# Graph attention layer after a masked attention layer: x1 gathered with (att + beta I) first, then the product with W, and token scores from x1 with a precomputed W a

## Chip, cores, metric

One core of a Trainium2 chip (trn2). The metric is device time in microseconds (us), median of several executions. Kernels are compared by the mean time of one kernel's fast runs over that of the other's fast runs of the same rounds, so a ratio is not quite the quotient of the medians quoted.

## The reference, cut to what matters

```python
# layer 0: 8-head attention over 256 tokens with an adjacency mask, residual, layer norm -> x1
x = _layernorm(x + _L0_gnn_ref(x, adj, Wq, bq, Wk, bk, Wv, bv, Wo, bo))
# layer 1, of x1 (64 batches, 256 tokens, 512 features)
h = jnp.einsum('bnc,cf->bnf', x, W)
s1 = jnp.einsum('bnf,f->bn', h, a1)
s2 = jnp.einsum('bnf,f->bn', h, a2)
e = jax.nn.leaky_relu(s1[:, :, None] + s2[:, None, :], negative_slope=0.2) * mask[None]
att = jax.nn.softmax(e, axis=2)
h_prime = jnp.einsum('bij,bjf->bif', att, h)
y = jax.nn.elu(h_prime + beta * h)
return _layernorm(x + y)
```

All is float32. With h = x1 W the layer is (att + beta I) x1 W, and s1 = x1 (W a1): that is what the change uses.

## The kernel before

Three batches are under way at a time. Each round of the loop runs the attention of one batch, the front (transposes, q, k, v) of the next and the back (projection, norm, layer 1, norm) of the one ahead, their steps merged by position: step i of a list of l steps stands at (i + 0.5) / l of the round.

```python
ps_mm = tile_pool(bufs=3, PSUM); ps_sc = tile_pool(bufs=2, PSUM); ps_tr = tile_pool(bufs=2, PSUM)

def merged(*lists):
    steps = [((i + 0.5) / len(l), k, f) for k, l in enumerate(lists) for i, f in enumerate(l)]
    return [f for _, _, f in sorted(steps, key=lambda s: s[:2])]

def layernorm(xt):                       # ... bn_stats, bn_aggr on VectorE
    nc.gpsimd.tensor_scalar(rs, mv[:, 1:2], EPS, None, ALU.add)
    nc.gpsimd.tensor_tensor(rs, rs, neg_half, ALU.pow)
    nc.vector.tensor_scalar(xt, xt, mv[:, 0:1], rs, ALU.subtract, ALU.mult)

def scores(t, g):                        # attention: 4 such steps a round
    for i in range(4): nc.tensor.matmul(ps[i % 2][...], QT..., KT...)       # two banks
    for s in range(2): nc.vector.tensor_add(pr[:, s::2, :], ps[s], mask)    # frees the banks
    nc.vector.tensor_reduce(nm, pr, AX.X, ALU.max, negate=True)
    for i in range(4): nc.scalar.activation(pr[:, i, :], ..., AF.Exp, bias=nm..., accum_out=sm...)
    nc.vector.reciprocal(rc, sm)
    nc.gpsimd.tensor_tensor(pr, pr, rc..., ALU.mult)    # 128x1024: "GpSimd's product" below
# flip(h): transposes of the probabilities, copied out by VectorE (even h) or ScalarE (odd h)
# mix(hp): two heads side by side, 4 matmuls of 64 columns of the array

def back(b):
    def proj(t):    # X += QT Wo, then
        layernorm(X[b][t])
    def flip(t):    # x1T = X transposed: 4 transposes and a copy
        transposed(X[b][t], t, x1T[0])
    def hidden(t):  # hs[t] = x1 W: 4 matmuls of 512 columns and a copy
        nc.scalar.copy(hs[t], ps)
        for i, v in enumerate((a1_sb, a2_sb)):
            nc.vector.scalar_tensor_tensor(junk, hs[t], 1.0, v, op0=ALU.mult, op1=ALU.mult,
                                           accum_out=s[t][:, i:i + 1])
    def edges(): ...      # s2 transposed on TensorE (tr_s), softmax of the edges over all engines
    def flip_att(): ...   # att transposed (tr_a)
    def last(t):    # ps = att hs, then
        nc.vector.scalar_tensor_tensor(u, hs[t], beta_sb, ps, op0=ALU.mult, op1=ALU.add)
        # ... elu(u), residual, layernorm, store
    return [proj, proj, flip, flip, hidden, hidden, edges, flip_att, last, last]   # for t = 0, 1
```

## Time and profile before

| | before |
|---|---|
| time | 3981.85 us (3980.74 to 3982.89, 4 runs) |
| a round of the loop | 61.44 us, 64 of them |
| TensorE busy | 94% |
| mean granted clock of TensorE | 0.945 |
| TensorE waits for the mask add ahead of a score step | 179.6 us, 2.87 us a round |

TensorE is busy almost always, and one wait stands out. The lines are in the prediction. A busy share counts modelled ends of pipelined instructions; for what an instruction costs on TensorE, the distance from its start to the next start is the better measure, and the one used here.

### The profile page before, as it was taken

The page shows a single profiled execution, that of the slowest core. Times are in us where ns is not written, and L with a number is a line of the kernel's source. Part 1 is how long each engine was busy: PE and PEld are TensorE (multiplying, and loading weights), DVE is VectorE, ACT ScalarE, POOL GpSimd, SP SyncE. Part 2 cuts the span into 40 slices and gives each one's busy share as a digit, 9 for nine tenths or more (in the row PEclk, how much of TensorE's full clock was granted, in tenths as well). Part 3 has the DMA queues.
Part 4 walks back from the last instruction along what each step waited for, and adds up shares of the span by engine and source line. Part 5 has one row for each costly group of instructions (what it writes and reads, how often), then busy time and mean ns, then how long its engine had stood idle before and what let it go on. Part 6 is the DMA issues. An engine that isn't in the chain of part 4 may idle for free.

```text
span 3978.9 us, 40466 instructions
## 1 busy us (share of the span) xinstructions
PE 3744.2 (94%) x15232; PEld 2258.9 (57%) x15232; DVE 2300.4 (58%) x4418; ACT 1147.1 (29%) x3265; POOL 924.5 (23%) x974
## 2 busy tenths in 40 slices
PE   7999999999999999999999999999999999999997
PEld 5555555556556555565555555555556556555563
DVE  3555565555655655656556555565555655655655
ACT  1332332322322323223222232332322322323222
POOL 2222221222222212222122222221222222212221
PEclk9999999999999999999999999999999999999998
DMA  2000000000000000000000000000000000000000
GB/s 93 13 20 22 11 22 16 17 22 11 22 22 11 22 16 17 22 11 22 20 14 22 14 19 22 11 22 16 16 22 11 22 22 11 22 17 16 16 6 16
DMA packets 40388, 76.26 MB, mean 19 GB/s; under 512 B 4352, under 2 KB 4608, under 8 KB 40192
## 3 DMA queue, kind: packets, MB, share of 16 engines
q1 hardware_dynamic: 37136, 67.39, 5.0%
q10 hardware_dynamic: 2640, 5.24, 0.4%
q8 instruction: 119, 1.95, 0.2%
q0 software_dynamic: 416, 1.05, 0.1%
q14 instruction: 77, 0.63, 0.1%
HBM read 40.11 MB, written 33.55 MB: 19 GB/s over the span
## 4 chain that ended last, share of the span: by engine, by line
PE 55%; DVE 22%; ACT 11%; POOL 7%; issue 4%; DMA 0%; POOLq 0%; SPq 0%; ACTq 0%; DVEq 0%
PE ps_qk L140 21%; PE ps_h L228 11%; ACT p L176 7%; PE tr_p L185 6%; PE ps_pv L197 5%; DVE nm L173 4%; PE ps_sc L168 4%; DVE x L120 3%; PE ps_g L269 3%; POOL rs L119 3%; PE tr_x L108 2%; DVE u L271 2%; DVE u L276 2%; DVE x L277 2%; DVE p L171 2%
## 5 line engine op out<-in xcount | busy, mean ns | idle before, releaser
L176 ACT ACTIVATE p<-p,nm 128x256 f32<-128x256 f32 x1024 | 507.6, 497 | 879.4 <-DVE nm L173 879.4
L179 POOL TENSOR_TENSOR p<-p,rc 128x1024 f32<-128x1024 f32 x256 | 484.6, 1893 | 903.8 <-DVE rc L178 903.8
L168 PE MATMUL ps_sc<-kT,qT 64*128 64x256 f32 x2048 | 388.2, 463 | 179.6 <-DVE p L171 179.6
L140 PE MATMUL ps_qk<-xT,wk_sb 128*128 128x256 f32 x2048 | 544.0, 413 | 0.0
L140 PE MATMUL ps_qk<-xT,wq_sb 128*128 128x256 f32 x2048 | 499.1, 387 | 0.3 <-ACT xT L109 0.3
L140 PEld LDWEIGHTS ps_qk<-xT,wk_sb 128*128 128x128 f32 x2048 | 417.3, 212 | 109.8 <-issue 53.5
L228 PE MATMUL ps_h<-w_sb,x1T 128*128 128x512 f32 x1024 | 473.1, 595 | 0.7 <-ACT x1T L109 0.7
L216 PE MATMUL ps_o<-wo_sb,qT 128*128 128x512 f32 x1024 | 460.8, 593 | 0.0
L146 PE MATMUL ps_v<-wv_sb,xT 128*128 128x512 f32 x1024 | 460.3, 592 | 0.0
L168 PEld LDWEIGHTS ps_sc<-kT,qT 64*128 64x128 f32 x2048 | 240.9, 215 | 351.6 <-DVE p L171 216.2
L140 PEld LDWEIGHTS ps_qk<-xT,wq_sb 128*128 128x128 f32 x2048 | 369.9, 190 | 85.8 <-issue 44.8
L120 DVE TENSOR_SCALAR x<-x,mv,rs 128x512 f32<-128x512 f32 x256 | 201.5, 787 | 316.7 <-POOL rs L119 316.7
L197 PE MATMUL ps_pv<-pT,v 128*64 128x256 f32 x2048 | 359.5, 393 | 0.3 <-DVE qT L199 0.3
L185 PE MATMUL tr_p<-ident,p 128*128 128x128 f32 x2048 | 350.8, 293 | 4.4 <-DVE pT L190 3.2
L190 DVE COPY pT<-tr_p 128x512 f32<-128x512 f32 x256 | 176.6, 690 | 306.4 <-PE tr_p L185 306.2
L171 DVE TENSOR_TENSOR p<-ps_sc,mask_sb 128x512 f32<-128x512 f32 x512 | 338.0, 672 | 22.8 <-PE ps_sc L168 22.8
L185 PEld LDWEIGHTS tr_p<-ident,p 128*128 128x128 f32 x2048 | 271.0, 151 | 117.4 <-issue 50.8
L146 PEld LDWEIGHTS ps_v<-wv_sb,xT 128*128 128x128 f32 x1024 | 194.4, 190 | 243.9 <-issue 243.9
L118 POOL TENSOR_SCALAR rs<-mv 128x1 f32<-128x1 f32 x256 | 56.1, 219 | 1113.1 <-DVE mv L116 1113.1
L173 DVE TENSOR_REDUCE nm<-p 128x4 f32<-128x1024 f32 x256 | 309.4, 1209 | 2.3
L246 POOL TENSOR_TENSOR e<-e,adj_sb 128x512 f32<-128x512 f32 x64 | 81.3, 1271 | 954.6 <-DVE e L245 954.6
L216 PEld LDWEIGHTS ps_o<-wo_sb,qT 128*128 128x128 f32 x1024 | 184.6, 190 | 185.2 <-issue 184.7
(56 smaller groups left out, 3746.1 us busy)
## 6 DMA issues: line engine op xcount, KB each, us to landing
x<-in_x_dram SPq DMA_DIRECT2D x128, 256.0 KB, 2.5
out_dram<-x SPq DMA_DIRECT2D x128, 256.0 KB, 2.0
wq_sb<-in_L_gnn_Wq_dram ACTq DMA_DIRECT2D x1, 1024.0 KB, 6.9
wk_sb<-in_L_gnn_Wk_dram ACTq DMA_DIRECT2D x1, 1024.0 KB, 14.6
wv_sb<-in_L_gnn_Wv_dram ACTq DMA_DIRECT2D x1, 1024.0 KB, 12.1
wo_sb<-in_L_gnn_Wo_dram ACTq DMA_DIRECT2D x1, 1024.0 KB, 8.6
w_sb<-in_L_gnn_W_dram ACTq DMA_DIRECT2D x1, 1024.0 KB, 9.9
a_sb<-in_L_gnn_a_dram POOLq DMA_DIRECT2D x2, 256.0 KB, 9.3
```

The lines of the kernel that those rows point to most:

```text
L120: nc.vector.tensor_scalar(xt, xt, mv[:, 0:1], rs, ALU.subtract, ALU.mult)
L140: nc.tensor.matmul(ps, w[:, c, m * P:(m + 1) * P], XT[b][:, c, :], start=c == 0, stop=c == C - 1)
L146: nc.tensor.matmul(ps, XT[b][:, c, t * P:(t + 1) * P], wv_sb[:, c, :], start=c == 0, stop=c == C - 1)
L168: nc.tensor.matmul(ps[i % 2][:, i // 2, :], QT[b][r:r + HD, h // 2, t * P:(t + 1) * P], KT[b][r:r + HD, h // 2, :], start=True, stop=True)
L171: nc.vector.tensor_add(pr[:, s::2, :], ps[s], mask_sb[:, t:t + 1, :].to_broadcast([P, 2, N]))
L173: nc.vector.tensor_reduce(nm, pr, AX.X, ALU.max, negate=True)
L176: nc.scalar.activation(pr[:, i, :], pr[:, i, :], AF.Exp, bias=nm[:, i:i + 1], accum_out=sm[:, i:i + 1])
L179: nc.gpsimd.tensor_tensor(pr, pr, rc.unsqueeze(2).to_broadcast([P, 4, N]), ALU.mult)
L185: nc.tensor.transpose(tr[:, k, t * P:(t + 1) * P], probs[t][:, h, k * P:(k + 1) * P], ident)
L197: nc.tensor.matmul(ps[s * HD:(s + 1) * HD, :], V[b][:, k, h * HD:(h + 1) * HD], pT[h][:, k, :], start=k == 0, stop=k == NT - 1)
L216: nc.tensor.matmul(ps, QT[b][:, c, t * P:(t + 1) * P], wo_sb[:, c, :], start=c == 0, stop=c == C - 1)
L228: nc.tensor.matmul(ps, x1T[0][:, c, t * P:(t + 1) * P], w_sb[:, c, :], start=c == 0, stop=c == C - 1)
```

## The change

The intent: spare the 8 transposes of x1 and the copies of h in each round by gathering x1 itself. TensorE can write (att + beta I) x1 straight in transposed form, which is what the product with W needs. The token scores then come from x1 and two vectors W a1, W a2 that are computed once. The diff, cut to its core (a helper line for each of beta_id and wa_sb, and removed comments, are left out):

```diff
+    wa_sb = const.tile([P, 2, C, P], F32, name="wa_sb")      # (W a1, W a2) on all partitions, once
 def proj(t):
     layernorm(X[b][t])
-def flip(t): ...
-def hidden(t): ...
+    for i in range(2):
+        nc.vector.scalar_tensor_tensor(junk, X[b][t], 1.0, wa_sb[:, i]..., accum_out=s[t][:, i:i + 1])
 def edges():
     nc.vector.tensor_scalar(e[:, t, :], e[:, t, :], rc[:, t:t + 1], None, ALU.mult)
+    nc.gpsimd.tensor_tensor(d, d, beta_id, ALU.add)          # d: the diagonal block of e
+def gather(g):                                               # y transposed: 4 matmuls of 256 columns
+    nc.tensor.matmul(ps[:, i, :], X[b][j][:, m * P:(m + 1) * P], att[1][:, j, :], ...)
+    nc.scalar.copy(yT[0][:, 2 * g:2 * g + 2, :], ps)
 def last(t):
-    nc.tensor.matmul(ps, att[1][:, j, t * P:(t + 1) * P], hs[j], ...)
-    nc.vector.scalar_tensor_tensor(u, hs[t], beta_sb, ps, op0=ALU.mult, op1=ALU.add)
+    nc.tensor.matmul(ps, yT[0][:, c, t * P:(t + 1) * P], w_sb[:, c, :], ...)
+    # relu, exp and max now read ps itself
-steps: proj, proj, flip, flip, hidden, hidden, edges, flip_att, last, last       (10)
+steps: proj, proj, edges, flip_att, gather, gather, last, last                   (8)
```

More of the change, by code (lines that the diff above doesn't have):

```diff
@@ L96, in gnn_two_layers @@
     beta_sb = on_all(beta, 0, 1, "beta_sb")
+    beta_id = const.tile([P, P], F32, name="beta_id")
+    nc.vector.tensor_scalar(beta_id, ident, beta_sb, None, ALU.mult)
     mask_sb = const.tile([P, NT, N], F32, name="mask_sb")
@@ L100, in gnn_two_layers @@
     nc.vector.tensor_scalar(mask_sb, mask_sb, NEG, None, ALU.mult)
+    wa_sb = const.tile([P, 2, C, P], F32, name="wa_sb")
+    for i, v in enumerate((a1_sb, a2_sb)):
+        row = ps_mm.tile([P, C, P], F32, tag="mm", name="ps_wa")
+        for c in range(C):
+            junk = work.tile([P, D], F32, tag="junk", name="junk")
+            col = small.tile([P, 1], F32, tag="wa", name="wa")
+            nc.vector.scalar_tensor_tensor(junk, w_sb[:, c, :], 1.0, v, op0=ALU.mult, op1=ALU.mult, accum_out=col)
+            nc.tensor.transpose(row[:, c, :], col.to_broadcast([P, P]), ident)
+        nc.scalar.copy(wa_sb[:, i], row)
     XT, QT, KT, V = {}, {}, {}, {}
@@ L210, in back @@
     def back(b):
-        hs, x1T, s, att = {}, {}, {}, {}
+        s, att, yT = {}, {}, {}
         def proj(t):
@@ L218, in proj @@
             layernorm(X[b][t])
-        def flip(t):
-            if t == 0:
-                x1T[0] = work.tile([P, C, N], F32, tag="x1T", name=f"x1T_{b}", bufs=1)
-            transposed(X[b][t], t, x1T[0])
-        def hidden(t):
-            ps = ps_mm.tile([P, D], F32, tag="mm", name="ps_h")
-            for c in range(C):
-                nc.tensor.matmul(ps, x1T[0][:, c, t * P:(t + 1) * P], w_sb[:, c, :], start=c == 0, stop=c == C - 1)
-            hs[t] = work.tile([P, D], F32, tag="h", name=f"h_{b}_{t}", bufs=4)
-            nc.scalar.copy(hs[t], ps)
             s[t] = small.tile([P, 2], F32, tag="s", name="s")
-            for i, v in enumerate((a1_sb, a2_sb)):
+            for i in range(2):
                 junk = work.tile([P, D], F32, tag="junk", name="junk")
-                nc.vector.scalar_tensor_tensor(junk, hs[t], 1.0, v, op0=ALU.mult, op1=ALU.mult,
-                                               accum_out=s[t][:, i:i + 1])
+                nc.vector.scalar_tensor_tensor(junk, X[b][t], 1.0, wa_sb[:, i].rearrange("p c k -> p (c k)"),
+                                               op0=ALU.mult, op1=ALU.mult, accum_out=s[t][:, i:i + 1])
         def edges():
@@ L255, in edges @@
                 nc.vector.tensor_scalar(e[:, t, :], e[:, t, :], rc[:, t:t + 1], None, ALU.mult)
+                d = e[:, t, t * P:(t + 1) * P]
+                nc.gpsimd.tensor_tensor(d, d, beta_id, ALU.add)
             att[0] = e
@@ L264, in flip_att @@
             nc.scalar.copy(att[1], tr)
-        def last(t):
-            ps = ps_mm.tile([P, D], F32, tag="mm", name="ps_g")
-            for j in range(NT):
-                nc.tensor.matmul(ps, att[1][:, j, t * P:(t + 1) * P], hs[j], start=j == 0, stop=j == NT - 1)
-            u = work.tile([P, D], F32, tag="u", name="u")
-            nc.vector.scalar_tensor_tensor(u, hs[t], beta_sb, ps, op0=ALU.mult, op1=ALU.add)
+        def gather(g):
+            if g == 0:
+                yT[0] = work.tile([P, C, N], F32, tag="yT", name=f"yT_{b}")
+            ps = ps_mm.tile([P, 2, N], F32, tag="mm", name="ps_y")
+            for i in range(2):
+                m = 2 * g + i
+                for j in range(NT):
+                    nc.tensor.matmul(ps[:, i, :], X[b][j][:, m * P:(m + 1) * P], att[1][:, j, :],
+                                     start=j == 0, stop=j == NT - 1)
+            nc.scalar.copy(yT[0][:, 2 * g:2 * g + 2, :], ps)
+        def last(t):
+            ps = ps_mm.tile([P, D], F32, tag="mm", name="ps_u")
+            for c in range(C):
+                nc.tensor.matmul(ps, yT[0][:, c, t * P:(t + 1) * P], w_sb[:, c, :], start=c == 0, stop=c == C - 1)
             m = work.tile([P, D], F32, tag="m", name="m")
-            nc.scalar.activation(m, u, AF.Relu, scale=-1.0)
+            nc.scalar.activation(m, ps, AF.Relu, scale=-1.0)
             nc.scalar.activation(m, m, AF.Exp, scale=-1.0)
-            nc.vector.scalar_tensor_tensor(u, u, 0.0, m, op0=ALU.max, op1=ALU.add)
-            nc.vector.scalar_tensor_tensor(X[b][t], u, -1.0, X[b][t], op0=ALU.add, op1=ALU.add)
+            nc.vector.scalar_tensor_tensor(m, ps, 0.0, m, op0=ALU.max, op1=ALU.add)
+            nc.vector.scalar_tensor_tensor(X[b][t], m, -1.0, X[b][t], op0=ALU.add, op1=ALU.add)
             layernorm(X[b][t])
             nc.sync.dma_start(out[b, t * P:(t + 1) * P, :], X[b][t])
-        steps = []
-        for f in (proj, flip, hidden):
-            steps += [lambda f=f, t=t: f(t) for t in range(NT)]
-        return steps + [edges, flip_att] + [lambda t=t: last(t) for t in range(NT)]
+        steps = [lambda t=t: proj(t) for t in range(NT)] + [edges, flip_att]
+        return steps + [lambda g=g: gather(g) for g in range(C // 2)] + [lambda t=t: last(t) for t in range(NT)]
     if B > 1:
```

## The prediction

> **What bounds the kernel now.** I read the page's engine totals, then the groups by form, then TensorE's timeline over several rounds of the loop, then the windows with the clock, then VectorE's timeline around the one stall that showed.
>
> ```profile
> PE 3744.2 (94%) x15232; PEld 2258.9 (57%) x15232; DVE 2300.4 (58%) x4418; ACT 1147.1 (29%) x3265; POOL 924.5 (23%) x974
> ...
> L168 PE MATMUL ps_sc<-kT,qT 64*128 64x256 f32 x2048 | 388.2, 463 | 179.6 <-DVE p L171 179.6
> ...
> L228 PE MATMUL ps_h<-w_sb,x1T 128*128 128x512 f32 x1024 | 473.1, 595 | 0.7 <-ACT x1T L109 0.7
> ```
>
> TensorE is the bound on average, but its only large idle time is 179.6 us ahead of the attention scores, waiting for VectorE to add the mask and so free the two score banks. The timeline shows this as one stall a round, always of the same length and 61.44 us apart:
>
> ```profile
> 2060.07 2.74 PE L168 MATMUL ps_sc<-kT,qT 64*128 64x256 f32 x8 [2.87 <-DVE p L171]
> 2121.51 2.73 PE L168 MATMUL ps_sc<-kT,qT 64*128 64x256 f32 x8 [2.87 <-DVE p L171]
> ```
>
> 64 rounds of 61.44 us are 3932 us; the other 50 us of the 3981.64 are start and end. The windows show that the stall costs more than its length (the column after POOL is the granted clock):
>
> ```profile
> 2056.00:2058.00 2.00, 1.20 (x6) 0.72 (x4) 1.97 (x3) 0.85 (x3) 0.00 (x0) 1.00 0.00 0
> 2058.00:2060.00 2.00, 0.00 (x0) 0.00 (x0) 1.18 (x4) 1.23 (x6) 0.48 (x1) 0.87 0.00 0
> 2060.00:2062.00 2.00, 1.93 (x7) 1.68 (x8) 0.68 (x3) 0.00 (x0) 1.92 (x3) 0.50 0.00 0
> 2062.00:2064.00 2.00, 2.00 (x9) 1.35 (x8) 1.72 (x3) 0.01 (x1) 0.25 (x1) 0.50 0.00 0
> 2064.00:2066.00 2.00, 2.00 (x8) 1.72 (x7) 2.00 (x4) 2.00 (x9) 0.00 (x0) 0.50 0.00 0
> 2066.00:2068.00 2.00, 2.00 (x14) 1.75 (x14) 1.80 (x4) 1.12 (x5) 1.65 (x1) 0.93 0.00 0
> ```
>
> From the fractions the half clock runs from 2059.5 to 2066.3. TensorE works through 6.2 us of it (2060.07 to 2066.3), so it loses 3.1 us. A round is then 55.4 us of work with its small gaps, 2.9 of stall and 3.1 of slow clock: 6 us, a tenth of the round, hangs on one wait. Its cause is on VectorE:
>
> ```profile
> 2045.77 1.55 DVE L120 TENSOR_SCALAR x<-x,mv,rs 128x512 f32<-128x512 f32 x1
> ...
> 2055.44 0.55 DVE L120 TENSOR_SCALAR x<-x,mv,rs 128x512 f32<-128x512 f32 x1 [2.71 <-POOL rs L119]
> 2055.91 1.21 DVE L173 TENSOR_REDUCE nm<-p 128x4 f32<-128x1024 f32 x1
> 2057.04 0.68 DVE L217 TENSOR_TENSOR x<-x,ps_o 128x512 f32<-128x512 f32 x1
> 2057.75 0.69 DVE L114 BATCH_NORM_STATS2 bn<-x 128x6 f32<-128x512 f32 x1
> 2059.26 0.18 DVE L178 RECIPROCAL rc<-sm 128x4 f32<-128x4 f32 x1 [0.82 <-ACT p L176]
> 2059.35 0.66 DVE L171 TENSOR_TENSOR p<-ps_sc,mask_sb 128x512 f32<-128x512 f32 x1
> ```
>
> In order, one score step's maximum waits behind a layer norm that waits 2.71 us for GpSimd; the exponentials wait for that maximum, the reciprocal for them, and the next mask add, which TensorE needs, stands behind the reciprocal. So the head of each round is a chain through VectorE; the rest of it is bound by TensorE.
>
> **What the Trainium skill says.** "TensorE: Matmul & The Clock Gate", Part 1, says the clock has two states, half and full, set by activity in free-running windows of about 3.4 us. The trace agrees: it falls to 0.50, and the drops at 2059.5, 339.2 and 219.7 us lie whole multiples of 3.413 us apart. An idle window of 2.28 us in 3.41 (67%) dropped the clock; the stall that ended at 278.85 lay across a window edge, 1.7 and 1.1 us, and the clock stayed at 1.00. The round of 61.44 us is also 18 such windows, so the kernel runs locked to the grid. The same page, section "Back-to-back issue gap", says that weight loads count as well as matmuls, and more at small widths; here 8 records of 256 columns take 1.73 us start to start and 8 of 512 take 3.43, and a 0.19 us load lies under each 0.216 us record, so halving the width costs nothing per column. "FP8 and Floating Point Precision", TensorE Precision Notes, says that true FP32 takes 4 passes; the trace agrees (a product of four 512-column matmuls, 3.43 us, is 16 times 0.214). "SBUF — State Buffer", section "Who interferes with whom", says that VectorE instructions with two SBUF inputs, or in the two-port mode, block against GpSimd; the norm's subtract and multiply shows it: 1.55 us beside a GpSimd add at 2045.77, 0.55 at 2055.44.
>
> **The change part by part, for one batch (a round).**
> TensorE: the 8 transposes of x1 go. Four take 0.44 us start to start (2006.12 to 2006.55), so 2 x 0.44 = 0.9 us. The product with W stays, 2 x 3.43 us. The product with the attention was 4 logical matmuls of 512 columns, 2 x 1.72 us; it becomes 8 of 256, 2 x 1.73. Net -0.9 us, all on the bound: 55.4 becomes 54.5.
> ScalarE: two copies of x1T (0.57) and two of h (0.59) go, two of yT (about 0.58, as other copies out of a bank) come: -1.2 us, on an engine that is 29% busy: nothing.
> VectorE: two beta*h+ps of 0.745 us go: -1.5 us. The two score reductions stay (0.69 + 0.08, twice for each block, 3.1 us) but move from the middle of the round, where VectorE idles, to straight behind the first norm, in the crowded head.
> GpSimd: two diagonal adds of 128x128 come, an estimate of 0.4 us each (a quarter of the 1.27 us of 128x512, plus a start cost), in the chain between the edges and the transposed attention.
> PSUM: the last product's bank is held through relu, exp and the max (0.63 + 0.63 + 0.69 us and queueing, about 3 us) instead of one read of 0.75. Between it and the third bank after it lie val, mix and the other last product, 3.4 + 1.0 + 3.4 us of TensorE: no wait expected.
> Order: the last stage loses 2 of 10 steps. By the program's spreading rule the second output projection now comes after the third score step, the edges right after the second projection's norm (between them q0, a score step, a flip and k0), and flip_att four steps on.
> Start: the new vectors W a need w_sb, issued at 18.2 us and landing 9.9 later, while the first q product ran at 21.05. If TensorE meets their transposes first, up to 13 us once; I take 10.
>
> **The head, walked by hand.** Relative to before: without the u instruction the last norm's VectorE work ends some 0.7 us earlier, before the first score step's mask add, not between its two halves beside GpSimd's bias add. The first maximum starts near 2046.5 instead of 2047.96, so everything up to the second mask adds comes 1.2 us earlier. The third score step is now only one transpose behind the second and waits about 0.5 us; the fourth, behind projection and q0 as before, waits about 1.2 us, plus 0.65 for its second bank. Against 2.87 + 0.65 before, that is better by about 1.2 us, and split. But then the edges need the second block's reductions, which stand in VectorE's queue behind the remaining score work: I expect 0 to 2.3 us of wait there, and 0 to 1.5 us at the transposed attention (its chain ran 5.9 us bare, 3918.22 to 3924.19, and has gained GpSimd work and busier neighbours). Sum of waits 2.5 to 6 us, middle 3.3, in three or four pieces. A piece over 2 us inside one window brings the half clock: 1.7 us for one window, 3.1 for two; middle 1.7.
> Round: 54.5 + 3.3 + 1.7 = 59.5 us; 64 x 59.5 = 3808, plus 50 and 10: **3868 us**, 2.9% less.
>
> **The rivals.**
> (a) The stalls split so that no window is mostly idle: 54.5 + 2.8 = 57.3 us, 3727 in all. For it: the stall at 278.85, and even a wait of 1.59 us ahead of the tr_p transposes at 284.98, left the clock at 1.00. Against: any one piece of 2 us undoes it.
> (b) The stall moves and the round stays locked at 18 windows, 61.44 us: about 3990 with the later start, so the saved 0.9 us is eaten. For it: the slow stretch ends on a grid edge wherever the stall lies, so a later stall end within it loses less clock, which pulls the round back to a multiple of 3.413. It needs waits and slow clock of 6.9 us together, which the walk reaches if the edges' wait is long.
> (c) VectorE becomes the head's bound: the work up to the transposed attention is, from the durations, about 25 us for VectorE against 19 for TensorE. Unless the order lets TensorE run q, k and flips ahead, two drops of clock follow and a round of 62.5 to 64: 4060 to 4160 us. Against: in the kernel before, such work did run ahead of the transposed attention, which waited 0.1 us.
> (d) Only the transposes count and stall and clock stay: 64 x 60.5 + 60 = 3932, within 2%.
>
> **Range and chances.** (a) at 25%, values between (a) and 3900 at 30%, (b) and (d) together at 33%, (c) at 12%. So faster by over 2% (under 3902) 0.55, within 2% 0.33, slower (over 4061) 0.12; range 3700 to 4000.
>
> **What would show it.** Right: no x1T transposes and TensorE's own work down by 0.9 us a round; product with attention 1.73 us per 8 records; waits of L168 split and shorter in total; granted clock above 0.945; first q product later by up to 13 us. The prediction is wrong if one new wait of over 3 us appears at the edges or the transposed attention, if the round is still 61.44 us, or if the product with the attention costs more per column than before.

## The result

| | before | after |
|---|---|---|
| time | 3981.85 us | 3966.69 us (3966.34 to 3967.94, 4 runs) |
| ratio | | 0.9963 (95%: 0.9949 to 0.9977) |
| mean round (59 rounds of the trace) | 61.42 us | 61.01 us |
| granted clock | 0.945 | 0.973 |
| wait ahead of score steps | 179.6 us | 29.3 us |
| wait ahead of the edge transposes | 1.9 us | 220.2 us |

The page's engine totals and two groups by form (columns: count, busy us, mean ns, then idle us before them and who ended it), of the kernel after:

```profile
PE 3637.0 (92%) x15240; PEld 2244.0 (57%) x15240; DVE 2231.8 (56%) x4307; ACT 1072.0 (27%) x3139; POOL 980.0 (25%) x1102
...
L181 PE MATMUL ps_sc<-kT,qT 64*128 64x256 f32 x2048 | 333.7, 402 | 29.3 <-DVE p L184 29.1
...
L241 PE MATMUL tr_s<-ident,s 128*128 128x128 f32 x128 | 40.2, 314 | 220.2 <-DVE junk L235 220.2
```

The wait that bounded the kernel before is nearly gone, and a larger one stands at the edges. TensorE's timeline after shows it in every round:

```profile
2006.50 0.32 PE L241 MATMUL tr_s<-ident,s 128*128 128x128 f32 x1 [3.38 <-DVE junk L235]
2067.77 0.32 PE L241 MATMUL tr_s<-ident,s 128*128 128x128 f32 x1 [3.37 <-DVE junk L235]
2127.98 0.48 PE L241 MATMUL tr_s<-ident,s 128*128 128x128 f32 x1 [3.37 <-DVE junk L235]
```

These two rounds take 61.27 and 60.21 us: the wait is always the same, the clock is not. The windows of after around the first of these waits (the granted clock is the third value from the end) show the half clock for about 3.4 us; around the second there is none.

```profile
2006.00:2008.00 2.00, 1.48 (x8) 1.03 (x9) 2.00 (x5) 0.00 (x0) 0.00 (x0) 1.00 0.00 0
2008.00:2010.00 2.00, 2.00 (x9) 1.53 (x8) 1.95 (x4) 1.47 (x5) 0.00 (x0) 0.52 0.00 0
2010.00:2012.00 2.00, 2.00 (x9) 1.86 (x8) 1.75 (x4) 1.09 (x6) 0.60 (x1) 0.62 0.04 8
...
2066.00:2068.00 2.00, 0.23 (x2) 0.23 (x3) 2.00 (x5) 0.00 (x0) 0.55 (x1) 1.00 0.00 0
2068.00:2070.00 2.00, 1.99 (x12) 1.48 (x12) 2.00 (x4) 0.34 (x1) 0.00 (x0) 1.00 0.00 0
```

What TensorE waits for is seen in the joined timeline of VectorE and GpSimd just ahead of the third one:

```profile
2118.83 1.28 DVE L184 TENSOR_TENSOR p<-ps_sc,mask_sb 128x512 f32<-128x512 f32 x2
...
2120.15 1.22 DVE L186 TENSOR_REDUCE nm<-p 128x4 f32<-128x1024 f32 x1
...
2121.28 0.68 DVE L230 TENSOR_TENSOR x<-x,ps_o 128x512 f32<-128x512 f32 x1
2122.00 0.69 DVE L127 BATCH_NORM_STATS2 bn<-x 128x6 f32<-128x512 f32 x1
...
2124.16 0.55 DVE L133 TENSOR_SCALAR x<-x,mv,rs 128x512 f32<-128x512 f32 x1 [0.99 <-POOL rs L132]
...
2124.71 0.66 DVE L184 TENSOR_TENSOR p<-ps_sc,mask_sb 128x512 f32<-128x512 f32 x1
2124.87 1.89 POOL L192 TENSOR_TENSOR p<-p,rc 128x1024 f32<-128x1024 f32 x1 [0.74 <-DVE rc L191]
2125.28 2.02 DVE L235 SCALAR_TENSOR_TENSOR junk<-x,wa_sb 128x512 f32<-128x512 f32 x1
2127.24 0.68 DVE L235 SCALAR_TENSOR_TENSOR junk<-x,wa_sb 128x512 f32<-128x512 f32 x1
```

This is one chain: the second projection (off TensorE at 2118.5), its residual and norm, then the two token-score reductions. The first reduction takes 2.02 us, the second, the same instruction, 0.68. The first begins 0.41 us after GpSimd's 1.89 us product has begun and ends 0.54 us after that product's end (2126.76): 1.3 us of the wait look like blocking, which the experiments test. The chain's first 2.7 us pass before the residual begins (2121.28): VectorE is at the mask adds and the maximum of the third score step. The chain takes 9.4 us, and TensorE has 5.6 us of other work and a wait of 0.46 us beside it; the rest is the 3.37 us.

### The profile page after: what moved, and what is told of

Its sections match the earlier page's. It is cut to its first block, busy times and chain, and to the rows that moved or that the text cites. A ratio compares the mean times of both kernels' runs of the same rounds, so it can differ in the third digit from the quotient of the medians.

```text
span 3964.6 us, 40122 instructions
## 1 busy us (share of the span) xinstructions
PE 3637.0 (92%) x15240; PEld 2244.0 (57%) x15240; DVE 2231.8 (56%) x4307; ACT 1072.0 (27%) x3139; POOL 980.0 (25%) x1102
## 4 chain that ended last, share of the span: by engine, by line
PE 69%; DVE 19%; POOL 7%; issue 3%; DMA 1%; ACT 0%; SPq 0%; POOLq 0%; DVEq 0%
PE ps_qk L153 17%; PE ps_u L285 11%; PE ps_v L159 11%; PE ps_pv L210 8%; DVE junk L235 6%; PE ps_y L278 6%; PE tr_p L198 6%; PE ps_o L229 5%; DVE p L184 3%; DVE nm L186 2%; DVE x L230 2%; POOL p L192 2%; POOL x L148 2%; POOL rs L132 2%; DVE x L133 2%
## 5 line engine op out<-in xcount | busy, mean ns | idle before, releaser
L153 PE MATMUL ps_qk<-xT,wq_sb 128*128 128x256 f32 x2048 | 560.1, 415 | 0.0
L153 PE MATMUL ps_qk<-xT,wk_sb 128*128 128x256 f32 x2048 | 488.4, 381 | 0.0
L153 PEld LDWEIGHTS ps_qk<-xT,wq_sb 128*128 128x128 f32 x2048 | 412.2, 210 | 103.2 <-issue 43.8
L285 PE MATMUL ps_u<-w_sb,yT 128*128 128x512 f32 x1024 | 466.7, 599 | 0.0
L153 PEld LDWEIGHTS ps_qk<-xT,wk_sb 128*128 128x128 f32 x2048 | 374.8, 193 | 40.7
L290 DVE SCALAR_TENSOR_TENSOR m<-ps_u,m 128x512 f32<-128x512 f32 x128 | 88.5, 691 | 540.8 <-ACT m L289 540.8
L198 PE MATMUL tr_p<-ident,p 128*128 128x128 f32 x2048 | 364.5, 300 | 30.1 <-POOL p L192 29.6
L181 PE MATMUL ps_sc<-kT,qT 64*128 64x256 f32 x2048 | 333.7, 402 | 29.3 <-DVE p L184 29.1
L288 ACT ACTIVATE m<-ps_u 128x512 f32<-128x512 f32 x128 | 76.4, 597 | 931.6 <-PE ps_u L285 931.6
L285 PEld LDWEIGHTS ps_u<-w_sb,yT 128*128 128x128 f32 x1024 | 189.3, 190 | 211.7 <-issue 184.5
L201 ACT COPY pT<-tr_p 128x512 f32<-128x512 f32 x256 | 150.1, 586 | 571.9 <-PE tr_p L198 571.9
```

Source lines behind the costliest of these rows:

```text
L153: nc.tensor.matmul(ps, w[:, c, m * P:(m + 1) * P], XT[b][:, c, :], start=c == 0, stop=c == C - 1)
L181: nc.tensor.matmul(ps[i % 2][:, i // 2, :], QT[b][r:r + HD, h // 2, t * P:(t + 1) * P], KT[b][r:r + HD, h // 2, :], start=True, stop=True)
L198: nc.tensor.transpose(tr[:, k, t * P:(t + 1) * P], probs[t][:, h, k * P:(k + 1) * P], ident)
L285: nc.tensor.matmul(ps, yT[0][:, c, t * P:(t + 1) * P], w_sb[:, c, :], start=c == 0, stop=c == C - 1)
```

## The experiments

Names: **theory A**, the edges merely stand too early; **theory B/C**, the amount of VectorE work at the head of the round is the bound, so a wait only moves; **theory D**, formed after eight runs, one chain (second projection to its reductions) with the blocking in it. "Slots" are positions in the round. In the new slots the projections stand at 0.0625 and 0.1875, so that the third score step comes ahead of the second projection; in the old slots, 0.05 and 0.15, it comes behind it. One thing must be known: the order on each engine is fixed when the kernel is built, by a pass that may move a step away from its slot. The order in the traces is what counts.

| run | what it is | us | ratio to before | mean round | work + waits + half clock | reduction, mean ns |
|---|---|---|---|---|---|---|
| before | | 3981.9 | | 61.42 | 55.5 + 2.9 + 3.1 | 693 |
| after | the change | 3966.7 | 0.9963 | 61.01 | 55.2 + 4.3 + 1.5 | 1011 |
| e1 | change, edges at 0.42 | 3958.4 | 0.9944 | 60.83 | 53.9 + 5.5 + 1.4 | 1012 |
| e2 | change, all old slots | 3750.4 | 0.9420 | 57.48 | 54.4 + 2.7 + 0.4 | 686 |
| e3 | before, no x1 transposes (wrong result) | 3913.0 | 0.9828 | 60.46 | 54.8 + 2.9 + 2.8 | |
| e4 | before, scores from x1 | 4004.2 | 1.0057 | 61.61 | 55.8 + 3.5 + 2.3 | 685 |
| e5 | change, projections in old slots | 3873.5 | 0.9726 | 59.43 | 55.1 + 3.3 + 1.0 | 684 |
| e6 | change, edges and on in old slots | 3853.9 | 0.9686 | 58.94 | 54.5 + 3.7 + 0.8 | 1008 |
| e7 | change, a score step moved ahead | 3992.4 | 1.0026 | 61.40 | 54.7 + 3.8 + 2.9 | 1008 |
| e8 | before, a score step moved ahead | 3835.3 | 0.9631 | 59.07 | 55.9 + 3.2 + 0.0 | 692 |
| e9 | change, GpSimd's product on ScalarE | 3809.5 | 0.9571 | 58.53 | 55.7 + 2.5 + 0.3 | 679 |
| e10 | change, short reductions (wrong result) | 3835.1 | 0.9636 | 58.93 | 54.2 + 3.9 + 0.8 | 220 |
| e11 | e2 with GpSimd's product on ScalarE | 3683.9 | 0.9253 | 56.37 | 54.4 + 1.8 + 0.2 | 684 |
| e12 | before, GpSimd's product on ScalarE | 3771.7 | 0.9474 | 58.05 | 56.3 + 1.7 + 0.0 | |

Mean rounds are taken from the first start of the projections over 59 rounds of the trace. The column after it splits them: TensorE's work (distances from start to start, weighted with the granted clock), its waits (idle times over 0.12 us), and the rest, lost to the half clock. A wait for the second bank inside a score step has no idle record of its own and counts as work. The last column is the mean duration of the 128x512 token-score reduction (128x64 in e10). The runs of e6 spread more than the others (3840.6 to 3864.0 us); its trace is of the fastest.

### e1: only the edges later

```diff
-slots of edges, flip_att, gather, gather: 0.3125, 0.4375, 0.5625, 0.6875
+slots of edges, flip_att, gather, gather: 0.42, 0.56, 0.65, 0.73
```

> The changed kernel with only the place of four steps altered: edges, flip_att and the two gather steps come later in the round (at 0.42, 0.56, 0.65, 0.73 of it, not 0.31 to 0.69); nothing else. Theory A (the lost gain is one wait: TensorE meets the edge transposes before the second block's reductions are done on VectorE): the 3.37 us wait at tr_s falls under 0.5 us, no half clock follows, the round goes from about 60.95 to 56.5-57.2 us, the whole to 3680-3730 us. Theory B (VectorE is the bound of the head as a whole, so the wait only moves): a wait of 2 us or more shows at the transposed attention or at q and k, the whole stays at 3880-3970 us.

The wait at the edges went (5.8 us over the whole run), and yet the time hardly moved. TensorE's timeline shows where it came back:

```profile
2005.02 1.11 PE L199 MATMUL tr_p<-ident,p 128*128 128x128 f32 x4 [2.52 <-DVE pT L204]
2015.06 0.74 PE L267 MATMUL tr_a<-ident,e 128*128 128x128 f32 x4 [1.74 <-POOL e L260]
```

The transposes of the probabilities wait 2.52 us for a copy out of their bank (L204), and that copy stands on VectorE behind the same 2.02 us reduction. Theory A falls: the edges were only the first to ask. A further 2.1 us a round (136.4 us in all) went at the transposed attention.

### e2: the change in the old slots

```diff
-slots: 0.0625, 0.1875, 0.3125, 0.4375, 0.5625, 0.6875, 0.8125, 0.9375
+slots: 0.05, 0.15, 0.65, 0.75, 0.79, 0.82, 0.85, 0.95
```

> The changed kernel with the two projections and the edges put back to the slots that they had before the change (0.05, 0.15; edges 0.65, flip_att 0.75). Theory A: no wait at the edges, but the wait ahead of the score step comes back (2 us or more, with the reductions now in the same queue 2.9 to 4.5), with the half clock: round 60 to 61.5 us, whole 3900 to 3990 us. If instead the order of projection and third score step does not matter and only the edges' place does: waits of scores under 1.5 us, whole 3680 to 3760 us.

3750.4 us, 5.8% under the kernel before: not theory A's figure, but the one for the case that the order of projection and third score step does not matter. It is the same algebra, so **the slots took the gain away**. By the table most of it is not work that the algebra spares: of the 3.9 us a round under the kernel before, 2.7 are half clock that went and 1.1 are work. The waits at score steps are 1.1 us a round (69.9 us in all); the edges no longer wait. But both groups of slots changed at once, and in this order the building pass had also moved one score step out of the head, so more runs were needed. e5 and e6 then showed that the projections' slots do matter.

### e3: what the transposes are worth alone

```diff
 def flip(t):
-    transposed(X[b][t], t, x1T[0])
+    x1T[0] = wq_sb[:, :, 0:N]      # wrong on purpose
```

> Wrong result on purpose: the kernel before without the 8 transposes of x1 a round and their two copies; the product with W takes a stretch of Wq in place of x1 transposed. Measures what the removed transposes are worth by themselves. If TensorE's work simply counts: 0.9 us a round, 3920 to 3930 us. If the round is held on the grid of the clock windows (61.44 us = 18 x 3.413): the round stays at 61.44 us and the whole within 0.3% of 3982 us, the saved work showing as more or longer half clock.

3913.0 us, ratio 0.9828: 67 us, or 1.0 us a round (61.42 to 60.46), slightly more than the 0.9 us worked out. The removed work counts, and the round is not held at a multiple of the clock's window. The stall of 2.87 us stayed.

### e4: only the token scores moved

```diff
 def proj(t):
     layernorm(X[b][t])
+    # the two reductions, of X with wa_sb
 def hidden(t):
-    # the two reductions, of hs with a1_sb, a2_sb
```

> The kernel before with one part of the change alone: the token scores are taken from x1 right after the first norm with the precomputed W a; h, the transposes of x1 and the slots stay as before. Theory A: moving 3.1 us of VectorE work into the head lengthens the wait ahead of the fourth score step from 2.87 to 3.3-5 us, no wait at the edges (they stay late); whole 4000 to 4120 us. Rival: the reductions fill idle time of VectorE, the wait stays 2.9 us, the whole at 3982 plus the later start of about 12: 3990 to 4000 us.

The stall ahead of the fourth score step grew from 2.87 to 3.18 us, a little less than I expected; the time by 0.57%, half of it the later start. In the old slots the reductions are not blocked (685 ns). So the moved VectorE work is by itself worth 0.3 us of stall, not 3: this speaks against the mere amount of work.

### e5 and e6: one half of the slots each

```diff
 e5: projections 0.05, 0.15; all else as in the change
 e6: edges and on 0.65, 0.75, 0.79, 0.82, 0.85, 0.95; projections as in the change
```

> The changed kernel with only the two projections back in their old slots (0.05, 0.15); edges and the rest as in the change; no score step leaves the head. Theory C, formed after the late-edges run: VectorE's queue at the head of the round is the bound, and a wait shows wherever TensorE first needs a late entry of it; the 3750 us run was fast since the ordering also moved one of the four score steps out of the head to the middle of the round. C expects here: waits of 3.5 us or more in sum, 3880 to 3990 us. If the slot of the projections is what counts: 3740 to 3800 us.

> The changed kernel with only edges and what follows in the old late slots (0.65 on); projections stay in the new slots, so the third score step stands ahead of the second projection. The instruction order shows one score step of the next batch in the middle of the round, as in the 3750 us run. Theory C: 3730 to 3800 us, no wait over 2 us. If the slot of the projections counts: 3880 us or more.

Neither fitted theory C, nor its rival, that the projections' slot alone counts. e5 gives 93 us and e6 113 us against the change; together 206, and e2, with both, gave 216. So the two halves add up like separate costs. The groups by form of the reductions, of after, e5 and e6 in turn, show the first one:

```profile
L235 DVE SCALAR_TENSOR_TENSOR junk<-x,wa_sb 128x512 f32<-128x512 f32 x256 | 249.7, 1011 | 0.1
```

```profile
L236 DVE SCALAR_TENSOR_TENSOR junk<-x,wa_sb 128x512 f32<-128x512 f32 x256 | 165.6, 684 | 0.1
```

```profile
L236 DVE SCALAR_TENSOR_TENSOR junk<-x,wa_sb 128x512 f32<-128x512 f32 x256 | 249.0, 1008 | 0.1
```

A mean of 1011 is one blocked at 2.02 us in four. With the projections in the new slots, the reductions of the second one meet GpSimd's product in every round (after, e1, e6, e7); in the old slots they do not (e2, e4, e5). In e6 the wait of 2.52 us at the transposes of the probabilities is there as in e1; in e5 the waits at the edges are 33.4 us in all. Yet the chain of e5 is not shorter (2006.2, the end of the second projection, to 2016.0: 9.8 us, unblocked); TensorE meets the edges later, after a wait of 1.67 us at the fourth score step, and its waits sum to 3.3 us a round in place of 4.3.

The second half has another source, which I had not looked for. TensorE's timeline of before around the transposed attention, and of e2 at the same place:

```profile
2028.44 0.65 PE L197 MATMUL ps_pv<-pT,v 128*64 128x256 f32 x2
2029.19 0.72 PE L262 MATMUL tr_a<-ident,e 128*128 128x128 f32 x4
...
2030.28 0.65 PE L197 MATMUL ps_pv<-pT,v 128*64 128x256 f32 x2
...
2036.59 1.08 PE L197 MATMUL ps_pv<-pT,v 128*64 128x256 f32 x4
2037.60 1.98 PE L269 MATMUL ps_g<-h,attT 128*128 128x512 f32 x4
```

```profile
2025.40 0.70 PE L182 MATMUL ps_sc<-kT,qT 64*128 64x256 f32 x4
2026.56 1.09 PE L211 MATMUL ps_pv<-pT,v 128*64 128x256 f32 x8 [0.45 <-DVE qT L213]
2027.58 0.70 PE L182 MATMUL ps_sc<-kT,qT 64*128 64x256 f32 x2
2028.83 0.74 PE L267 MATMUL tr_a<-ident,e 128*128 128x128 f32 x4 [0.55 <-POOL e L260]
...
2029.94 0.70 PE L182 MATMUL ps_sc<-kT,qT 64*128 64x256 f32 x2
```

A mix is four matmuls on half of the array's columns. Uncut it takes 1.02 us to the next start (2026.56 to 2027.58). In the kernel before and in the change, the order cuts one mix a round into pieces of one, one and two matmuls. The last pair alone takes 1.01 us (2036.59 to 2037.60), as long as all four uncut, and the two single ones 0.75 and 0.58 us to the next start. (Some records are missing in the counts of such lines; the pieces are known from the built order.) By start-to-start sums over a round the mixes take 5.2 us after and 4.1 us in e2 and e6 (and 5.4 before): the cut costs 1.2 to 1.3 us a round. But the order of e2 and e6 cuts a score step (ps_sc) in its place: its three pieces above take 0.71, 0.70 and 0.62 us without the waits, 2.0 us in place of 1.06 uncut, and the score steps of a round go from 4.9 to 5.9 us. So the cut mix does not account for the 113 us of e6: the two nearly cancel. In e1, e7 and e10 no mix is cut either, so these runs do not change one thing alone.

### e7 and e8: one score step moved into the round before

```diff
-attention(i - 1): scores(0, 0) first in round i
+scores(0, 0) of batch i at 0.66 of round i
```

> The changed kernel with every slot as it is, only the first score step of each batch put into the preceding round (at 0.66 of it). Theory C: VectorE's head gets 2.7 us shorter, the wait at the edges falls from 3.37 to 0.5-1.5 us, the half clock mostly goes: 3680 to 3790 us. Theory A (the place of the edges alone): the wait stays at 3 us or more, 3930 us or more.

> The kernel before with the same single move: first score step of each batch in the preceding round. Theory C: the wait of 2.87 us ahead of the fourth score step falls under 1.3 us and the half clock goes in most rounds: 3670 to 3780 us. Rival: that wait comes from the norm's wait for GpSimd between two score steps, not from the amount of work, and stays over 2 us: 3930 us or more.

In the change it did nothing for the wait, though it took a quarter of the score work out of the head:

```profile
2013.04 0.47 PE L242 MATMUL tr_s<-ident,s 128*128 128x128 f32 x1 [3.37 <-DVE junk L236]
2074.48 0.47 PE L242 MATMUL tr_s<-ident,s 128*128 128x128 f32 x1 [3.38 <-DVE junk L236]
```

The same 3.37 us: the wait is the length of a chain that begins at the second projection, and work ahead of that does not matter. Theory C falls in the form that any VectorE work of the head counts; VectorE work inside the chain, as that of the third score step, was not tested. The run got slower since nearly every round now stood so in the clock's windows that some 7 us ran at half clock. In the kernel before the same move did help (ratio 0.9631, less than I had expected): the stall of 2.87 became 0.77, 1.59 and 0.69 us at three places, and the clock rose from 0.945 to 0.996. The waits of a round did not shrink (2.9 to 3.2 us); split, they no longer brought the half clock, and that is the whole gain.

### e9 and e10: the blocking, and the reductions

```diff
 e9:  -nc.gpsimd.tensor_tensor(pr, pr, rc..., ALU.mult)
      +for i in range(4): nc.scalar.activation(pr[:, i, :], pr[:, i, :], AF.Copy, scale=rc[:, i:i + 1])
 e10: -reductions over X[b][t] (512 features)
      +reductions over X[b][t][:, 0:64]      # wrong on purpose
```

> The changed kernel with one thing taken off GpSimd: the 1.89 us product of the probabilities with the reciprocal sums is done by four ScalarE instructions. Theory D, formed after the eight runs so far: the wait at the edges is the length of one chain, second projection to its reductions (about 9.5 us with 6.1 us of TensorE work beside it), and 1.34 us of it is the first reduction standing blocked beside that GpSimd product (2.02 us in place of 0.68). D expects the reduction at 0.68, the wait at tr_s down from 3.37 to 1.5-2.1 us, 3800 to 3890 us. Rival (the head's amount of VectorE work decides): VectorE's work is the same, the wait stays over 2.8 us, 3920 us or more.

> Wrong result on purpose: the changed kernel with the two token-score reductions over 64 of the 512 features, all else equal. Theory D: the second reduction and half of the first leave the chain, though the first still stands behind the GpSimd product: wait at tr_s 1.8-2.6 us, 3830 to 3920 us. If the blocking is not real (the 2.02 us is only its own work): the wait falls to under 1 us, 3700 to 3790 us. If neither reduction is on the chain: unchanged, 3950 us or more.

e9 is the test of theory D. TensorE's and VectorE's timelines of e9:

```profile
2043.66 0.32 PE L242 MATMUL tr_s<-ident,s 128*128 128x128 f32 x1 [2.10 <-DVE junk L236]
...
2101.98 0.32 PE L242 MATMUL tr_s<-ident,s 128*128 128x128 f32 x1 [2.10 <-DVE junk L236]
```

```profile
2042.33 0.66 DVE L236 SCALAR_TENSOR_TENSOR junk<-x,wa_sb 128x512 f32<-128x512 f32 x1
...
2042.92 0.68 DVE L236 SCALAR_TENSOR_TENSOR junk<-x,wa_sb 128x512 f32<-128x512 f32 x1
```

The first reduction takes 0.66 us in place of 2.02, the wait fell from 3.37 to 2.10 us, by 1.27 of the 1.36 that the reduction got shorter, and the clock rose to 0.993, since most rounds now ran without the half clock (58.3 us; some took 59.8). The time, 3809.5 us, is in the range expected, and ScalarE at 39% took the work without becoming a bound. (Part of the 157 us is not this wait: with GpSimd free, the other short waits, such as 29.6 us ahead of the transposes of the probabilities, went too, and the half clock fell by 1.2 us a round. The building pass also moved one matmul of a score step, which added some 0.6 us of work.)

e10 gave the time expected, 3835.1 us, but not quite as expected. The wait at the edges fell to 1.01 us, and 1.48 us stood at the transposes of the probabilities right behind it; the reductions (220 ns) were not blocked. The blocking had not gone, though: it had moved one instruction ahead, to the norm's subtract, which takes 2.11 us beside GpSimd's product in 63 rounds and 0.55 us elsewhere:

```profile
2055.87 1.90 POOL L192 TENSOR_TENSOR p<-p,rc 128x1024 f32<-128x1024 f32 x1
2055.93 2.11 DVE L133 TENSOR_SCALAR x<-x,mv,rs 128x512 f32<-128x512 f32 x1 [0.61 <-POOL rs L132]
2058.08 0.22 DVE L235 SCALAR_TENSOR_TENSOR junk<-x,wa_sb 128x64 f32<-128x64 f32 x1
```

So e10 agrees with the blocking. Its time proves little on the reductions: the waits of a round fell only from 4.3 to 3.9 us, the work by 1.0 us, since no mix is cut in its order, and the half clock by 0.7.

### e11 and e12: best version, and before with the same help

```diff
 e11: e2 with the edit of e9        e12: before with the edit of e9
```

> The change's algebra in the old slots (the 3750 us version) with the probabilities' product on ScalarE too. Theory D: the norm's own GpSimd steps no longer queue behind that product (waits of 1.5 and 1.6 us for them before the subtract), so the wait of 1.09 us ahead of the fourth score step and the one at the flips shrink and the half clock goes in most rounds: 3620 to 3720 us. Rival (ScalarE, now with eight instructions of 0.5 us a score step, becomes the chain): no gain, 3740 us or more.

> The kernel before with only the probabilities' product moved to ScalarE. If the wait of 2.87 us ahead of the fourth score step is the norm waiting for GpSimd behind that product (2.71 us in the trace), it falls to 0.5-1.5 us and the half clock goes: 3660 to 3800 us, and the change's own worth is then the difference from the run of the change in the old slots with the same move (0.9 to 1.6 us a round, 60 to 100 us). If it is the amount of VectorE work: wait over 2 us, 3930 us or more.

e12: the stall ahead of the fourth score step fell from 2.87 to 0.58 us with the norm's wait for GpSimd (2.71 to 0.42 us), and the half clock went from these rounds (0.996). So that stall was the norm queueing behind GpSimd's product. e11 is the fastest version found and correct: 3683.9 us, 7.5% under the kernel before. The wait of 1.09 us ahead of its fourth score step did not shrink as I had expected; what went is the waits at the probabilities (the granted clock is 0.990 in both). From e12 to e11 is 88 us, 1.7 us a round with 12.3 us of later start against it: what the change is worth with its slots put right and GpSimd out of the way. In this e3's transposes are 1.0 us and the mix that is no longer cut 1.3 us by the start-to-start sums, while the score step that is cut instead takes 1.0 us back; the rest was not taken apart. The two cuts come from the order and not from the algebra.

## Why the prediction was right or wrong

**What bounds the kernel before:** right as far as the wait's cost and place go; e12 confirms the cause that it named, the norm waiting for GpSimd.

**TensorE's own work, -0.9 us:** right for the transposes. e3 measured 1.0 us, and the gather took 3.56 us a round against 3.54 for the product that it replaces, so half the width costs nothing per column. By the sums of the table the whole work fell by only 0.25 us a round (55.45 to 55.20). Some 0.5 us of the difference is an estimate of how it is counted: the instruction before a wait counts to its modelled end (an edge transpose 0.27 us in place of 0.11, the transposes of x 0.65 in place of 0.49), and the change has three waits a round where the kernel before had one.

**Minor terms:** the first q product came at 32.55 in place of 21.05 us, 11.5 us later (10 taken); the diagonal adds took 0.45 us each (0.4); the last bank, held longer, made no wait.

**The head, up to the fourth score step:** the third score step waited 0.45 us (0.5 said) and 0.65 for its second bank; the fourth did not wait at all (1.2 said).

**The step that failed:** "then the edges need the second block's reductions, which stand in VectorE's queue behind the remaining score work: I expect 0 to 2.3 us of wait there", and with it "Sum of waits 2.5 to 6 us, middle 3.3". The mechanism was right, the size was not: 3.37 us every round. Without the blocking (e9) it is 2.10 us, inside the range given. With 0.45 and 0.65 at the third score step (a wait like the last one was already inside the 55.4 us of work, so the prediction's sum counts it twice), 0.46 at the transposes of the probabilities and up to 0.44 at the transposed attention, the waits of a round came to 4.9 to 5.4 us. Missing were 1.3 us of blocking. I had quoted the skill that an instruction with two SBUF inputs blocks against GpSimd, and used it for the norm alone; the moved reductions are such instructions, and their new place is beside GpSimd's product. In the old place, behind hidden, they met none (693 ns).

**The half clock:** 1.7 us said, 1.5 us lost on average: right. (A round without it, 60.21 us, was only 0.8 us under the mean, as it waited 0.44 us at the transposed attention instead.) The limit said, a piece over 2 us inside one window, did not hold: between 200 and 3650 us of the trace of after all 50 drops came after windows with 1.8 us or more of idle time, 1.82 the least, and in e2 twelve came after windows with 1.1 us. So the round of 54.5 + 3.3 + 1.7 = 59.5 us became 55.2 + 4.3 + 1.5 = 61.0, the 0.65 us of the second bank now counted in the 55.2.

**Rivals:** (b), that a new wait eats the gain, is what came, but not by locking: the rounds were 60.2 to 61.3 us, and e3 shows that saved work shortens them. (c) was wrong in its form: the rounds stayed under 62.5 us, and e7 shows that the amount of VectorE work ahead of the chain was not it. (a), 3727 us, needs waits that are short, and e2 comes near it.

**Where the expected gain went:** by the sums of the table, TensorE's work fell by 0.25 us a round and the half clock by 1.6, but the waits grew by 1.4: the old wait of 2.87 us went, and 3.37 us at the edges with two short ones came. Most of that is the chain from the second projection to its reductions, which got into TensorE's way because dropping two steps moved the slots of the other eight. Put back, the same algebra gives 5.8%. Not all of this is the algebra's: the kernel before gains 3.7% by a moved score step alone (e8), and where both have GpSimd's product on ScalarE the change is worth 88 us, 2.3%.

**Open:** how the 113 us of the edges' slots divide between shorter waits (0.6 us a round), less half clock (0.7) and less work (0.7, with the mix uncut and a score step moved and cut); no run kept all but one of these. It is also open why windows with so little idle time as in e2 brought the half clock.

## What to carry to other kernels

When steps are dropped from an interleaved schedule, the ones that stay move: first run the new algebra in the old slots, then tune the slots. A reduction moved off a quiet place must be priced where it lands: name every GpSimd instruction that will run beside it. Follow a wait back to where its chain begins before moving the one that waits: here e1 moved the waiting step, and the wait went to the next one in line. Weigh waits with the clock that they bring: e8 waits longer in sum than the kernel before and is 147 us faster.

## What the Trainium skill lacked or had wrong

- "TensorE: Matmul & The Clock Gate", Part 1, gives the window (about 3.4 us) and the two states, and the traces agree; it names at least one idle window as what brings the half clock, and here windows that were idle in part did. In the kernel before 2.28 of 3.41 us (67%) did and 1.7 us did not; in the change all 50 drops between 200 and 3650 us came after 1.82 us or more, and windows of up to 1.75 us brought none; but in e2 twelve came after 1.1 us, so idle time alone does not decide. It does not say either that a loop can settle on the grid: nearly all rounds of before and of e7 were 61.44 us, 18 windows, those of e3 were not.
- The same page, Part 4, tells of about 275 ns for a transpose inside a kernel (it names bf16; here it is float32). The trace's durations are near it (293 ns for the transposes of the probabilities), but start to start four took 0.44 us, 0.11 us each, and that is about what removing them gave back (e3).
- "SBUF — State Buffer", section "Who interferes with whom", states the blocking that was met and was right, in its size too: it says that the later one fully blocks. 1.48 us were left of GpSimd's product when the reduction began; with its own 0.68 us that makes 2.16 us, and 2.02 was measured.
- No page that I read has a figure for cutting a group of half-array matmuls; it would belong in "TensorEngine Tiling (Array Packing)". Here four took 1.02 us uncut, two of them alone 1.01 us, and a score step of 1.06 us took 2.0 in three pieces.
